# A deformable convolution with fewer columns in its edge tiles, and another order of work for its first image

## The chip, the cores and the metric

The kernel runs on one core of a Trainium2 chip. The metric is the device time of one execution in microseconds (us). The profile comes from one execution of its own. The engines are named as in the profile: PE (TensorE; PEld is its weight load), DVE (VectorE), ACT (ScalarE), POOL (GpSimd) and SP (SyncE, which here only issues DMAs).

## What is computed

Eight images of 128 channels and 64 x 64 pixels pass two layers. The first is a deformable convolution behind a group norm: an ordinary 3 x 3 convolution gives, for each pixel and each of nine taps, an offset in y, one in x and a mask; each tap then samples the image at its shifted place with bilinear weights, and a 1 x 1 product per tap sums the samples. The second layer is a mixture of four 3 x 3 convolutions, and the change doesn't touch it. Cut to what matters:

```python
def _deform_conv(x, off_w, off_b, w, b):
    om = conv(x, off_w, pad=1) + off_b[None, :, None, None]      # 27 rows
    off = om[:, :2 * KK].reshape(B_, KK, 2, H_, W_)
    mask = jax.nn.sigmoid(om[:, 2 * KK:])
    py = off[:, :, 0] + (jnp.arange(H_) - 1.0)[:, None] + ky
    px = off[:, :, 1] + (jnp.arange(W_) - 1.0)[None, :] + kx
    y0, x0 = jnp.floor(py), jnp.floor(px)
    ly, lx = py - y0, px - x0
    val = corner(y0, x0, (1 - ly) * (1 - lx)) + corner(y0, x0 + 1, (1 - ly) * lx) \
        + corner(y0 + 1, x0, ly * (1 - lx)) + corner(y0 + 1, x0 + 1, ly * lx)
    val = val * mask[:, None]
    return einsum('bckhw,ock->bohw', val, w) + b      # then batch norm, relu

x = x + _L0_conv_ref(_gn(x), ...)     # the deformable layer
x = x + _L1_conv_ref(_gn(x), ...)     # the mixture of experts
```

## The kernel before

Sampling is done as a matrix product. An image has 11 bands of T = 6 rows (NT1 = 11), a band 11 tiles of 6 columns. A tile looks at a window of Q = 10 by 10 pixels (6 and a reach of 2 to each side), which makes QQ = 100 rows of a contraction. Each of its 6 x 6 base positions has nine taps: 324 columns. The weight of a window pixel for a column is a product of two "tents", one of the y distance (times the mask) and one of the x distance.

The tables. `tables(b)` (L230) is a generator that makes the tents of image b, and the main loop takes a step of it at each tile (two at each third), so that its work lies between the tiles of an earlier image. For image 0 it runs to its end before the first tile (L622). It loads the image (L245), normalises it (L257 to L286), and computes the offset convolution in `combine` (L312, DVE) and `tap` (L329, PE); the result is `om`. ACT makes a copy of it with x and y exchanged (L375). Both are written to DRAM, by row (L378) and by column (L382), and read back (L397 for y offsets and masks, L405 for x offsets) with one image row or column per partition, a tap's values shifted by its place, into parts of the tile combo1. Then come five steps i, one for each pixel distance: ACT makes x tents in two instructions (L453 Abs, L460 Relu), DVE y tents in three (L458, L461, L463), and SP stores both to the DRAM tables taby and tabx (`store`, L431).

The bands. `load_y` (L471, six DMAs a band, POOL) and `load_x` (L485, ten DMAs) fetch a band's tents with each row repeated for the window pixels. `pick` (L503, ACT) cuts the windows out of the image, and `pixels` (L521) turns them on PE (L529) and copies them out of PSUM on ACT (L536). There is one PSUM buffer for this, ps_t. `weights` (L540, DVE) multiplies tents of x and y to `s`, three tiles ahead. `sample` (L554) multiplies window by weights on PE (L557) into one of three PSUM buffers `pq`, and ACT copies that to the tile `samples` (L563), which the convolution product of the band before reads (`conv`, L572, nine of 384 columns). A copy on ACT (L665) carries two rows from one band's samples to the next. Convolved rows go to DRAM (L590).

The order is the program's own: instructions stand on each engine in the order in which the loop at L640 issues them, and a DMA on SP, ACT or POOL also waits for the eighth DMA before it of its kind. The column order of a tile is (tap, row, column): `x_wts` is read with a step over base columns a, and y with step 1:

```python
x_wts[g % 3][0:QQ, c].rearrange("p a k r -> p k r a"),
y_wts[g % 2][0:QQ, :, :, T * c : T * c + T].rearrange("p r k a -> p k r a"),
```

Base positions run over 66 x 66 and not 64 x 64, since a tap's row and column are put at the place the convolution will ask for. So at an image's border some taps of the outermost base positions are computed and never read.

Of the kernel before, what the change touches and what calls it, by code (L numbers as in the profile page):

```python
# [16 lines left out]
P = 128  # L17
# [3 lines left out]
TAPS = 9  # L21
# [36 lines left out]
def deform_moe_conv(  # L58
# [110 lines left out]
    def dense():  # L169

        with ExitStack() as st:
# [15 lines left out]
            for t in picked:  # L187
# [18 lines left out]

            combos = [a1.tile([P, H // 2, W], F32, name=f"combo{i}") for i in range(2)]
# [3 lines left out]
                    "p (u v j) -> p u v j", u=3, v=3  # L211
                )
                for i in range(2)
            )
            off_x = flat[0:WB, 2 * YSTEP : 2 * YSTEP + TAPS * (WP6 - 1) + ROWPAD]


            x_wts = [a1.tile([P, NT1, T, TAPS, T], F32, name=f"xwts{i}") for i in range(3)]
            y_wts = [a1.tile([P, T, TAPS, WB], F32, name=f"ywts{i}") for i in range(2)]
# [3 lines left out]
            samples = [a1.tile([P, TAPS, T + 2, WB], F32, name=f"samples{i}") for i in range(2)]  # L223
            dw_sb = a1.tile([P, TAPS, P], F32, name="dw_sb")
            ystats = a1.tile([P, B, NT1, 6], F32, name="ystats")
            ymvs = a1.tile([P, B, 2], F32, name="ymvs")
            xts, ss = {}, {}
            bands = [(b, j) for b in range(B) for j in range(NT1)]

            def tables(b):  # L230
# [11 lines left out]
                others = (nc.sync, nc.sync) if b else (nc.scalar, nc.gpsimd)  # L242
# [132 lines left out]
                nc.scalar.copy(omc, omr.rearrange("p (h w) -> p w h", w=W))  # L375
                yield from pause(4)
                for j in range(4):
                    nc.sync.dma_start(  # L378
                        out=rowwise[b][:, j * HW // 4 : (j + 1) * HW // 4],
                        in_=omr[32 * j : 32 * j + 27],  # L380
                    )
                    others[j % 2].dma_start(  # L382
                        out=colwise[b][:, :, H // 4 * j : H // 4 * (j + 1)],
                        in_=omc[32 * j + 9 : 32 * j + 18],
                    )
# [3 lines left out]
                if b == 0:  # L389
                    for t in (y_wts[1], x_wts[1], x_wts[2]):  # L390
                        nc.vector.memset(t, 0.0)
                yield from pause(9)
                for k in range(3):
                    rows = slice(k, k + H)
                    for t, c in ((off_y, 3 * k), (mask, 2 * TAPS + 3 * k)):
                        one = t[rows, 0, k, 0:1]
# [3 lines left out]
                                ap=[list(one.ap[0]), [3 * WB + 1, 3], [1, W]],  # L400
# [3 lines left out]
                    one = off_x[rows, k * 3 * (WP6 - 1) + ROWPAD :]  # L404
                    others[k % 2].dma_start(  # L405
                        out=bass.AP(
                            tensor=one.tensor, offset=one.offset,
                            ap=[list(one.ap[0]), [WP6, 3], [1, H]],
# [9 lines left out]
                else:  # L418
                    tents = []
                    for t in samples:  # L420
                        flat = t.rearrange("p k r w -> p (k r w)")
# [4 lines left out]
                by_bands = bass.AP(  # L426
                    tensor=one.tensor, offset=one.offset,
                    ap=[list(one.ap[0]), [T, NT1], [WP6 - 1, TAPS], [1, T]],
                )

                def store(i):  # L431
# [8 lines left out]
                    )  # L440
                    nc.sync.dma_start(
# [8 lines left out]
                for i in range(NR):  # L450
                    ty, tx = tents[0][i], tents[1][i]
                    step = steps[0:WB, i : i + 1]
                    nc.scalar.activation(  # L453
                        tx.rearrange("p (n k j) -> p n k j", n=NT1, j=T), by_bands, AF.Abs, bias=step
                    )

                    dy, at = off_y.rearrange("p u v j -> p (u v j)"), REACH - i
                    nc.vector.tensor_scalar(ty, dy, -1.0, float(1 - at), ALU.mult, ALU.add)  # L458
                    yield
                    nc.scalar.activation(tx, tx, AF.Relu, bias=1.0, scale=-1.0)  # L460
                    nc.vector.scalar_tensor_tensor(ty, dy, float(1 + at), ty, ALU.add, ALU.min)  # L461
                    yield
                    nc.vector.scalar_tensor_tensor(  # L463
                        ty, ty, 0.0, mask.rearrange("p u v j -> p (u v j)"), ALU.max, ALU.mult
                    )
                    if i:
                        store(i - 1)
                    yield from pause(2)
                store(NR - 1)

            def load_y(g, r, engine):  # L471

                if g >= len(bands):
# [3 lines left out]
                    out=y_wts[g % 2][r * Q : (r + NR) * Q, r].rearrange("p b c -> p (b c)"),  # L477
# [62 lines left out]
            def weights(n):  # L540

                if n >= len(bands) * NT1:
                    return
                g, c = divmod(n, NT1)
                s = a6.tile([P, TAPS, T, T], F32, name="s")
                nc.vector.tensor_tensor(  # L546
                    s[0:QQ],
                    x_wts[g % 3][0:QQ, c].rearrange("p a k r -> p k r a"),
                    y_wts[g % 2][0:QQ, :, :, T * c : T * c + T].rearrange("p r k a -> p k r a"),
# [4 lines left out]
            def sample(n):  # L554
                g, c = divmod(n, NT1)
                pq = ps_q.tile([P, TAPS, T, T], F32, name="pq")
                nc.tensor.matmul(  # L557
                    pq.rearrange("p k r a -> p (k r a)"),
                    lhsT=xts[g][0:QQ, c],
                    rhs=ss.pop(n)[0:QQ].rearrange("p k r a -> p (k r a)"),  # L560
                    start=True, stop=True,
                )
                nc.scalar.copy(samples[g % 2][:, :, 2 : T + 2, T * c : T * c + T], pq)  # L563

            def conv(g, i, py):
# [4 lines left out]
                n = 3 * kx + ky  # L570
# [4 lines left out]
                    rhs=samples[g % 2][:, n, first + ky : T + ky, kx : kx + W],  # L575
# [16 lines left out]
            LOADS = 17  # L592
            made, later = tables(0), tables(1)
            for _ in range(LOADS):
                next(made)
            nc.sync.dma_start(out=offw_sb[:, :, 0:27], in_=off_w)
            for j in range(4):
                nc.sync.dma_start(
                    out=offb_sb[32 * j : 32 * j + 27], in_=off_b.rearrange("a s -> s a")
                )  # L600
            def reach():
# [5 lines left out]
                count = a1.tile([1, 1], F32, name="count")  # L607
                nc.vector.tensor_reduce(count, pn[0:1], AX.X, ALU.add)
                nc.vector.tensor_copy(count_i, count)
# [5 lines left out]
            for u in offu_sb:  # L615
                nc.gpsimd.tensor_scalar(u, u, 0.5, None, ALU.mult)
# [5 lines left out]
            for _ in made:  # L622
                pass
# [621 lines left out]
```

## Time and profile before

| | |
|---|---|
| three executions | 1700.83, 1702.66, 1706.56 us |
| the profiled execution | 1705.5 us, of which the span of the instructions is 1703.8 |
| PE busy in the span | 1591.8 us (93%) |
| DVE, ACT, POOL busy | 1280.1, 954.9, 938.3 us |
| sampling matmuls (L557, PE) | 1936 records, 693.5 us: two passes for each of 968 tiles |
| convolution matmuls (L572, PE) | 1584 records, 624.4 us |
| tile weights (L546, DVE) | 968 of 761 ns |
| copies out of PSUM (L563, ACT) | 968 of 443 ns |
| granted TensorE clock, mean | 0.973 |

A group's line in the profile names source line, engine, operation, what is written and read, the shape, how often, busy time and the mean of one; behind the bar stands the time for which the engine was idle before these instructions, and what ended the wait. A matmul of this data type is recorded twice, once for each pass, and the records of consecutive matmuls overlap, so that the distance from start to start tells more than the length. In an answer by windows each row is a stretch of time with the busy time of each engine in it.

### The profile page before, as it was taken

The page shows a single profiled execution, that of the slowest core. Times are in us where ns is not written, and L with a number is a line of the kernel's source. Part 1 is how long each engine was busy: PE and PEld are TensorE (multiplying, and loading weights), DVE is VectorE, ACT ScalarE, POOL GpSimd, SP SyncE. Part 2 cuts the span into 40 slices and gives each one's busy share as a digit, 9 for nine tenths or more (in the row PEclk, how much of TensorE's full clock was granted, in tenths as well). Part 3 has the DMA queues.
Part 4 walks back from the last instruction along what each step waited for, and adds up shares of the span by engine and source line. Part 5 has one row for each costly group of instructions (what it writes and reads, how often), then busy time and mean ns, then how long its engine had stood idle before and what let it go on. Part 6 is the DMA issues. An engine that isn't in the chain of part 4 may idle for free. (4 is left out here: it accounts for less than half of the span.)

```text
span 1703.8 us, 20572 instructions
## 1 busy us (share of the span) xinstructions
PE 1591.8 (93%) x6106; PEld 918.3 (54%) x6106; DVE 1280.1 (75%) x1990; ACT 954.9 (56%) x1970; POOL 938.3 (55%) x1518
## 2 busy tenths in 40 slices
PE   3299999999999999999999999999999479999998
PEld 1155565666566556656665665566665234444443
DVE  6586777678687868776786878686664888888882
ACT  1465765776576667657765766676664423333320
POOL 3375576658667757766686676667771412222210
PEclk9599999999999999999999999999999689999999
DMA  4644864685477457647854775675762624444111
GB/s 133 128 119 113 166 169 114 143 183 132 112 159 183 115 120 184 154 114 141 192 125 110 161 183 126 129 162 133 171 149 53 266 87 155 158 153 149 76 63 52
DMA packets 197598, 235.82 MB, mean 138 GB/s; under 512 B 133964, under 2 KB 148048, under 8 KB 197478
## 3 DMA queue, kind: packets, MB, share of 16 engines
q0 software_dynamic: 94976, 124.94, 33.4%
q1 hardware_dynamic: 100556, 109.04, 21.6%
q8 instruction: 54, 0.88, 0.2%
q10 hardware_dynamic: 1946, 0.41, 0.1%
q14 instruction: 66, 0.54, 0.1%
HBM read 183.00 MB, written 50.82 MB: 137 GB/s over the span
## 5 line engine op out<-in xcount | busy, mean ns | idle before, releaser
L546 DVE TENSOR_TENSOR s<-xwts,ywts 100x324 f32<-100x324 f32 x968 | 706.6, 761 | 205.3 <-PE pq L557 172.3
L557 PE MATMUL pq<-s,xt 100*128 100x324 f32 x1936 | 693.5, 440 | 6.0 <-DVE s L546 6.0
L563 ACT COPY samples<-pq 128x324 f32<-128x324 f32 x968 | 425.1, 443 | 410.1 <-PE pq L557 403.5
L572 PE MATMUL py<-samples,dw_sb 128*128 128x384 f32 (+1 forms) x1584 | 624.4, 476 | 0.7 <-ACT y L583 0.7
L492 POOL DMA_DIRECT2D xwts<-tabx x863 | 524.7, 618 | 74.0 <-DMA ywts<-taby 35.9
L476 POOL DMA_DIRECT2D ywts<-taby x528 | 302.9, 588 | 337.2 <-DVE s L546 259.6
L557 PEld LDWEIGHTS pq<-s,xt 100*128 100x128 f32 x1936 | 324.5, 190 | 163.5 <-issue 28.7
L572 PEld LDWEIGHTS py<-samples,dw_sb 128*128 128x128 f32 x1584 | 299.9, 189 | 135.1 <-ACT y L583 2.7
L529 PE MATMUL pt<-ident,picked 128*100 128x128 f32 x968 | 194.6, 276 | 44.2 <-ACT picked L516 34.6
L529 PEld LDWEIGHTS pt<-ident,picked 128*100 128x100 f32 x968 | 121.0, 128 | 186.9 <-issue 44.8
L1159 PE MATMUL pc<-v,u 128*128 128x512 f32 x384 | 172.5, 598 | 9.3 <-DVE u L1108 9.3
L1159 PE MATMUL pc<-v,wmix 128*128 128x512 f32 x384 | 176.0, 604 | 0.0
L536 ACT COPY xt<-pt 100x512 f32<-100x512 f32 (+1 forms) x264 | 147.7, 559 | 2.2 <-PE pt L529 2.2
L1159 PEld LDWEIGHTS pc<-v,u 128*128 128x128 f32 x384 | 72.4, 190 | 98.3 <-issue 85.1
L1137 ACT ACTIVATE t<-pc,bmix 128x512 f32<-128x512 f32 x32 | 22.0, 687 | 182.3 <-PE pc L1159 100.3
L586 DVE BATCH_NORM_STATS2 ystats<-y 128x6 f32<-128x384 f32 (+1 forms) x88 | 48.3, 549 | 100.4 <-ACT y L583 100.4
L1159 PEld LDWEIGHTS pc<-v,wmix 128*128 128x128 f32 x384 | 72.3, 191 | 88.4 <-issue 84.7
L508 ACT COPY picked<-pad 128x900 f32<-128x900 f32 x88 | 91.6, 1041 | 9.6 <-DMA xwts<-tabx 9.6
L665 ACT COPY samples<-samples 128x1188 f32<-128x1188 f32 x80 | 95.9, 1199 | 0.0
L987 POOL TENSOR_TENSOR x<-x,xt 128x512 f32<-128x512 f32 x32 | 47.3, 1514 | 85.0 <-ACT x L985 85.0
L312 DVE TENSOR_TENSOR combo<-pad 128x1024 f32<-128x1024 f32 x64 | 77.4, 1227 | 8.5 <-PE pc L329 8.5
L987 POOL TENSOR_TENSOR pad<-pad,pad 128x512 f32<-128x512 f32 x28 | 39.6, 1445 | 71.7 <-ACT pad L985 71.5
(145 smaller groups left out, 998.3 us busy)
## 6 DMA issues: line engine op xcount, KB each, us to landing
ywts<-taby POOLq DMA_DIRECT2D x528, 116.0 KB, 4.2
pad<-in_x_dram SPq DMA_DIRECT2D x48, 512.0 KB
xwts<-tabx POOLq DMA_DIRECT2D x173, 116.0 KB, 4.1
out_dram<-yo SPq DMA_DIRECT2D x32, 512.0 KB
xwts<-tabx POOLq DMA_DIRECT2D x172, 92.8 KB, 4.0
yd<-y SPq DMA_DIRECT2D x80, 192.0 KB
xwts<-tabx POOLq DMA_DIRECT2D x173, 69.6 KB, 3.7
pad<-yd SPq DMA_DIRECT2D x16, 512.0 KB
```

What stands on the lines that cost most here:

```text
L476: engine.dma_start(out=y_wts[g % 2][r * Q : (r + NR) * Q, r].rearrange("p b c -> p (b c)"), in_=bass.AP(tensor=y_table[b].tensor, offset=y ...
L492: engine.dma_start(out=x_wts[g % 3][q:QQ:Q, :, lo:hi].rearrange("p t a b c -> p t (a b c)"), in_=bass.AP(tensor=x_table[b].tensor, offset= ...
L508: nc.scalar.copy(picked[g % 2][:, 1 : NT1 - 1], bass.AP(tensor=one.tensor, offset=one.offset, ap=[list(one.ap[0]), [T, NT1 - 2], [W, Q], [ ...
L529: nc.tensor.transpose(pt[0:QQ, c], picked[g % 2][:, c0 + c].rearrange("p y x -> p (y x)"), ident,)
L536: nc.scalar.copy(xts[g][0:QQ, c0 : c0 + n], pt[0:QQ, 0:n])
L546: nc.vector.tensor_tensor(s[0:QQ], x_wts[g % 3][0:QQ, c].rearrange("p a k r -> p k r a"), y_wts[g % 2][0:QQ, :, :, T * c : T * c + T].rear ...
L557: nc.tensor.matmul(pq.rearrange("p k r a -> p (k r a)"), lhsT=xts[g][0:QQ, c], rhs=ss.pop(n)[0:QQ].rearrange("p k r a -> p (k r a)"), star ...
L563: nc.scalar.copy(samples[g % 2][:, :, 2 : T + 2, T * c : T * c + T], pq)
L572: nc.tensor.matmul(py[:, first:], lhsT=dw_sb[:, 3 * ky + kx], rhs=samples[g % 2][:, n, first + ky : T + ky, kx : kx + W], start=(i == 0), ...
L665: nc.scalar.copy(samples[g % 2][:, :, 0:2], samples[(g - 1) % 2][:, :, T : T + 2])
L987: adder.tensor_tensor(y, y, xt[:, c * CH : (c + 1) * CH], ALU.add)
L1159: nc.tensor.matmul(pc, lhsT=us[j][:, kx], rhs=vs[g][:, rows, kx : kx + W], start=(kx == 0), stop=(kx == 2),)
```

## The change

It has two parts. Every tile's columns get another order: (row, tap row) by (base column, tap column), with the tap column innermost, in tables, weights and PSUM. With the taps in reverse order (the weights and biases of the offset convolution are reversed by small copies at the start), the columns at the border that nobody reads lie at the ends, and `sample` leaves them out: a tile in the first or last band has two of 18 rows fewer, one at the left or right end two of 18 columns fewer. The copy to `samples` exchanges the last two dimensions, so that the samples of one tap lie side by side along w, and at the ends it takes a second, small copy. The last y tent step becomes three instructions, one for each tap column.

The second part is for image 0: the loads of offsets and masks go to places that don't overlap; the x offsets all come on ACT's queue; the exchange copy is shared by ACT and DVE; the sigmoid's table is loaded at the start; the x tents of the first three bands come first and have stores of their own; the y tables are stored alone; the x loads of band 0 are issued before the last y tent, `pick` and `pixels` of band 0 before the rest; and the stores of the other x tents stand between the x loads of band 1.

```diff
-                    "p (u v j) -> p u v j", u=3, v=3
+                    "p (v u j) -> p v u j", u=3, v=3
...
+            tent_y = combos[0].rearrange("p h w -> p (h w)")[0:WB, 0:YSTEP]
...
-            x_wts = [a1.tile([P, NT1, T, TAPS, T], F32, name=f"xwts{i}") for i in range(3)]
-            y_wts = [a1.tile([P, T, TAPS, WB], F32, name=f"ywts{i}") for i in range(2)]
+            x_wts = [a1.tile([P, NT1, T, T, TAPS], F32, name=f"xwts{i}") for i in range(3)]
+            y_wts = [a1.tile([P, T, 3, WB, 3], F32, name=f"ywts{i}") for i in range(2)]
...
-            samples = [a1.tile([P, TAPS, T + 2, WB], F32, name=f"samples{i}") for i in range(2)]
+            samples = [a1.tile([P, T + 2, 3, 3, WB], F32, name=f"samples{i}") for i in range(2)]
...
+            nc.scalar.activation(count_f, nhalf[0:1], AF.Sigmoid)
...
-                others = (nc.sync, nc.sync) if b else (nc.scalar, nc.gpsimd)
+                beside = nc.sync if b else nc.gpsimd
...
-                nc.scalar.copy(omc, omr.rearrange("p (h w) -> p w h", w=W))
+                turned = omr.rearrange("p (h w) -> p w h", w=W)
+                if b:
+                    nc.scalar.copy(omc, turned)
+                else:
+                    nc.scalar.copy(omc[:, 0 : W // 2], turned[:, 0 : W // 2])
+                    nc.vector.tensor_copy(omc[:, W // 2 :], turned[:, W // 2 :])
...
-                    rows = slice(k, k + H)
+                    rows = slice(2 - k, 2 - k + H)
...
-                by_bands = bass.AP(
+                by_bases = bass.AP(
                     tensor=one.tensor, offset=one.offset,
-                    ap=[list(one.ap[0]), [T, NT1], [WP6 - 1, TAPS], [1, T]],
+                    ap=[list(one.ap[0]), [1, WB], [WP6 - 1, 3], [3 * (WP6 - 1), 3]],
                 )
...
+                def tent_y_of(i):
+                    for v in range(3):
+                        nc.vector.scalar_tensor_tensor(
+                            tents[0][i].rearrange("p (v j u) -> p v j u", v=3, u=3)[:, v],
+                            tent_y.rearrange("p (v u j) -> p v j u", u=3, v=3)[:, v], 0.0,
+                            mask[:, v].rearrange("p u j -> p j u"), ALU.max, ALU.mult,
+                        )
...
+                early, rest = slice(0, FIRST * T), slice(FIRST * T, WB)
+                for i in range(NR):
+                    distance_x(i, early)
+                    tent_x(i, early)
+                for i in range(NR):
+                    for _ in distance_y(i):
+                        pass
+                    tent_y_of(i)
+                    store_y(i)
+                    if i == 1:
+                        for n in range(FIRST):
...
+                            nc.sync.dma_start(out=bass.AP(...), in_=bass.AP(...))
+                    if i == NR - 2:
+                        for q in range(5):
+                            load_x(0, q, nc.gpsimd if q % 2 else nc.sync)
+                for q in range(5, Q):
+                    load_x(0, q, nc.sync)
+                pick(0)
+                for _ in pixels(0):
+                    pass
+                for i in range(2):
+                    distance_x(i, rest)
+                    tent_x(i, rest)
+                for r in range(T):
+                    load_y(0, r, nc.gpsimd if r < 4 else nc.scalar)
+                pick(1)
+                for i in range(2, NR):
+                    distance_x(i, rest)
+                    tent_x(i, rest)
+                nc.vector.memset(x_wts[2], 0.0)
+                for r in range(T):
+                    load_y(1, r, nc.gpsimd)
+                for q in range(Q):
+                    load_x(1, q, nc.sync)
+                    if q % 2:
+                        i = q // 2
+                        nc.sync.dma_start(...)
...
-                    x_wts[g % 3][0:QQ, c].rearrange("p a k r -> p k r a"),
-                    y_wts[g % 2][0:QQ, :, :, T * c : T * c + T].rearrange("p r k a -> p k r a"),
+                    x_wts[g % 3][0:QQ, c].rearrange("p a r (y x) -> p (r y) a x", x=3),
+                    y_wts[g % 2].rearrange("p r y a x -> p (r y) a x")[
+                        0:QQ, :, T * c : T * c + T
+                    ],
...
+                asked = (
+                    slice(None),
+                    slice(2 * (j == 0), 3 * T - 2 * (j == NT1 - 1)),
+                    slice(2 * (c == 0), 3 * T - 2 * (c == NT1 - 1)),
+                )
+                pq = ps_q.tile([P, 3 * T, 3 * T], F32, name="pq")
                 nc.tensor.matmul(
-                    pq.rearrange("p k r a -> p (k r a)"),
+                    pq[asked],
                     lhsT=xts[g][0:QQ, c],
-                    rhs=ss.pop(n)[0:QQ].rearrange("p k r a -> p (k r a)"),
+                    rhs=ss.pop(n)[0:QQ].rearrange("p m a x -> p m (a x)")[asked],
                     start=True, stop=True,
                 )
-                nc.scalar.copy(samples[g % 2][:, :, 2 : T + 2, T * c : T * c + T], pq)
+                rows = samples[g % 2].rearrange("p r y x w -> p (r y) x w")
+                by_columns = pq.rearrange("p m (a x) -> p m x a", x=3)
+                m0, m1 = 2 * (j == 0), 3 * T - 2 * (j == NT1 - 1)
+                parts = [(slice(0, 3), int(c == 0), T - (c == NT1 - 1))]
+                if c == 0:
+                    parts.append((slice(2, 3), 0, 1))
+                if c == NT1 - 1:
+                    parts.append((slice(0, 1), T - 1, T))
+                for x, lo, hi in parts:
+                    nc.scalar.copy(
+                        rows[:, 6 + m0 : 6 + m1, x, T * c + lo : T * c + hi],
+                        by_columns[:, m0:m1, x, lo:hi],
+                    )
...
-                    rhs=samples[g % 2][:, n, first + ky : T + ky, kx : kx + W],
+                    rhs=samples[g % 2][:, first + ky : T + ky, 2 - ky, 2 - kx, kx : kx + W],
...
+            FIRST = 3
...
+            nc.sync.dma_start(out=raw_w.rearrange("p k s t -> p k (s t)"), in_=off_w)
+            nc.sync.dma_start(out=raw_b.rearrange("p s t -> p (s t)"), in_=off_b)
...
+            for k in range(TAPS):
+                nc.scalar.copy(reversed_w[:, :, :, k], raw_w[:, :, :, TAPS - 1 - k])
+            for k in range(TAPS):
+                nc.scalar.copy(reversed_b[:, :, k], raw_b[:, :, TAPS - 1 - k])
             for j in range(4):
+                nc.sync.dma_start(out=offb_sb[32 * j : 32 * j + 27], in_=offb_row)
...
-                nc.gpsimd.tensor_scalar(u, u, 0.5, None, ALU.mult)
+                nc.scalar.activation(u, u, AF.Copy, scale=0.5)
```

## The prediction

> **What bounds the kernel now.** I read the page's 40 slices first, then the windows by stage, the timeline of one steady band, the windows of the eleven bands of one image, and last the timeline of the start.
>
> ```profile
> PE   3299999999999999999999999999999479999998
> ```
>
> Two slices (85 us) at the start in which TensorE hardly works, then thirty full ones. The windows by stage:
>
> ```profile
> core 0: us, PE busy (x) PEld busy (x) DVE busy (x) ACT busy (x) POOL busy (x), PEclk, DMA share, GB/s
> 0.00:32.80 32.80, 16.13 (x100) 6.64 (x100) 20.02 (x30) 4.90 (x6) 12.20 (x38) 1.00 0.45 150
> 32.80:75.50 42.70, 3.07 (x11) 1.78 (x11) 20.04 (x20) 15.05 (x22) 11.81 (x20) 0.54 0.58 110
> 86.20:1306.00 1219.80, 1211.30 (x5119) 745.82 (x5118) 924.66 (x1371) 811.55 (x1754) 813.14 (x1372) 1.00 0.63 143
> ```
>
> From 86 to 1306 us PE is busy 99.3%: it is the bound of the banded stage. From 32.8 to 75.5 nothing is busy for even half the time: that is a chain of latencies. After 1306 the change touches nothing. In a steady band:
>
> ```profile
> 601.26 0.71 PE L557 MATMUL pq<-s,xt 100*128 100x324 f32 x2
> 601.81 0.81 PE L572 MATMUL py<-samples,dw_sb 128*128 128x384 f32 x2
> 602.46 0.38 PE L529 MATMUL pt<-ident,picked 128*100 128x128 f32 x2
> ```
>
> Starts count here, since ends overlap. 324 columns take 0.55 us until the next start, 384 take 0.65: 1.69 ns a column for both passes, with no fixed part. Fewer columns are time. Now bands 1, 6, 7, 8, 9 of image 3:
>
> ```profile
> 559.00:570.70 11.70, 11.31 (x53) 8.31 (x52) 9.96 (x18) 10.54 (x23) 9.18 (x14) 1.00 0.44 107
> 635.30:648.40 13.10, 13.10 (x53) 8.43 (x52) 9.75 (x16) 10.39 (x24) 10.75 (x19) 1.00 0.82 163
> 648.40:661.60 13.20, 13.20 (x53) 8.36 (x52) 12.58 (x21) 11.74 (x25) 6.66 (x12) 1.00 0.65 149
> 661.60:675.40 13.80, 13.19 (x52) 8.31 (x51) 11.07 (x17) 9.84 (x23) 9.24 (x16) 1.00 0.97 212
> 675.40:688.50 13.10, 13.10 (x53) 8.42 (x52) 8.54 (x13) 8.58 (x21) 7.79 (x13) 1.00 0.90 224
> ```
>
> The fourth figure is ACT: 8.6 us in a plain band, 11.74 in the band that also makes tents, of 13.1 that PE needs. ACT is second everywhere, and full in one band of an image; PE idles only there and in band 1 (0.6 and 0.4 us). The start:
>
> ```profile
> 45.64 0.47 DVE L458 TENSOR_SCALAR samples<-combo 66x594 f32<-66x594 f32 x1 [0.45 <-issue]
> 57.35 0.29 SPq L433 DMA_DIRECT2D taby<-samples  x1
> 58.67 18.54 SPq L492 DMA_DIRECT2D xwts<-tabx  x14
> 62.56 3.43 POOL L476 DMA_DIRECT2D ywts<-taby  x6 [19.70 <-DMA tabx<-samples]
> 75.49 4.73 DVE L546 TENSOR_TENSOR s<-xwts,ywts 100x324 f32<-100x324 f32 x7 [18.16 <-DMA ywts<-taby]
> ```
>
> Tents from 45.6, last y store 57.4, first y load 62.6, first weights 75.5.
>
> [...] L546 (x read with a step of 54 words) takes 761 ns for 324 elements, while contiguous L1107 takes 552 for 384; and ACT shows the like, since L375 (step 64) takes 2.00 us for 1024 elements where L665 takes 1.20 for 1188. [...]
>
> **The change, part by part.**
>
> *Columns.* An edge tile asks 288 of 324 columns, and a corner 256. Of 121 tiles of an image, 9 bands lose 2 x 36 = 72 columns, the first and last 9 x 36 + 2 x 68 = 460: 1568 an image, 12,544 in all, times 1.69 ns = 21.1 us off PE. PE being the bound, all of it is on the path unless another engine now ends later.
>
> *Weights on DVE (L546).* x now comes in runs of three and the output stays contiguous; [...]I take 0.57. That is 11 x 0.19 = 2 us of DVE a band, hidden behind PE: no time won.
>
> *y tents on DVE.* The last step becomes three of 198 elements with both sources hopping[...], overlapping to 1.35, in place of 0.69 (start to start). Five an image cost 3.3 us, about 2.3 in the tent band; DVE there stands at 12.58 and loses 2 through the weights: 12.9 under PE's 13.0. Nothing, narrowly.
>
> *x distances on ACT.* They now read with a step of 207 words: from L375 (2.00 - 0.2)/1024 = 1.76 ns an element against 0.83, so 0.82 becomes 1.37 us. Four fall in the tent band: +2.2. The edge tiles' extra copies (16 or 18 elements; L516's 70 cost 0.15 start to start) add 0.3. ACT there: 11.74 + 2.2 + 0.3 = 14.2 against PE's 13.1: 1.1 late. The pixel transposes have one PSUM buffer, so a late ACT stops PE soon (today's 0.6 us idle is just that wait, on ACT xt L536). I charge 1.1 us in each of the 7 images that make tents for a later one: +8.
>
> *The sample copies on ACT (L563).* They now read PSUM with a step of three words, 968 times. Below: 0.44 us as today. Above: every element pays what an SBUF hop costs ACT, 324 x 0.93 = +0.30, 0.74 us. Below today is excluded, since today's read is contiguous. I take 0.44: TensorE writes those words in this trace at one per 0.84 ns a pass[...]. It is a judgement; the upper end makes the main rival.
>
> *The first image.* Up to the offsets (32.8 us) little moves: eighteen small copies on ACT (about 0.15 us each) must wait for off_w, then four bias DMAs for them, and the first combine on DVE (15.39) for those DMAs, because they read combos[0]. With off_w there by 9.5, copies to 12.3, issue and landing 3.5 us, it is 0 to 0.7 late. The six offset and mask loads no longer wait for one another (36.6 to 44.9 today with gaps): issued by 41.5, landed by 43.5, y tents from 43 instead of 45.6. Each now takes 2.66 us instead of 2.0: the last at 43 + 13.3 = 56.4, not 57.3. So this is worth only 1 us. What follows is worth more: no x store lies in front of the last y store, which needs about 3.2 us instead of 5.2 (the first, alone, took 2.1), so y loads begin at 59.7; nine x loads stand in SP's queue before or beside it and are out by then. Four y loads on POOL and two on ACT are issued in 2.4 us and land 4 to 5.7 later: first weights at 66.5 against 75.5, that is 9 us. Queued behind on SP: ten x loads of band 1 and five x stores, 15 x 0.8 = 12 us from 61 plus 4 to land, 77; band 1 asks for them at 66.5 + 10.3 = 76.8. ACT's late distances (five of 1.7 us, the last ending about 68) hold up the first sample copies by under 1 us. I take 8.5 off, with 3 to 12 as bounds.
>
> *Sum.* -21.1 + 8 - 8.5 = -21.6. The profiled execution took 1705.5 us (span 1703.8 and 1.7 around it): 1684. The three runs have a median of 1702.66, 0.17% less: 1681.
>
> **Rivals.**
>
> *A, the sum above*: 1681, chance 0.40. *B, the tent band holds*: ACT's excess is taken up by the bands beside it (8.5 of 13) and the 8 us don't come: 1673; for it, PE waits little on ACT today; against it, the single transpose buffer. 0.15. *C, the start gives little*: the longer DVE tents, or SP's queue, where a DMA waits for the eighth before it and landings take 6.9 us (the median under load), eat most of it; column gain and stalls stand: 1690. 0.13.
>
> *D, the copies cost something*, 0.55 us: 1.2 us more ACT a band. Band 1 is then at 10.54 + 0.3 + 1.2 = 12.0 against 11.2, band 7 at 15.4 against 13.1; 3.1 an image, 22 in seven; -21.1 + 22 - 8.5: 1695. 0.12.
>
> *E, ACT becomes the bound (slower).* One mechanism: the PSUM read with a step pays the full hop, 0.74 us. Then a band carries 3.3 + 0.3 more: band 1 14.1 against 11.2, band 6 14.0 against 13.0, band 7 17.5 against 13.1, band 8 (with one late distance) 14.0 against 13.1; 9.2 us an image, 64 in seven; -21.1 + 64 - 8.5 = +35: 1738. It decides from about +0.16 us a copy (0.60), where 4.2 us an image eat up the 29.6 won. For it: both other engines' rows show what hops cost; against it: those are SBUF rows. 0.20.
>
> **How the numbers follow.** Predicted: 1681, with its own range of 1672 to 1692. A to D hold 0.80 of the chance and their tails lie outside, so the range reaches into E's lower part: 1666 to 1725. About 0.3% (5 us) is what a measurement of this kernel can tell from no change. Faster: A, B, C and most of D, 0.75; same: the rest of D, 0.05; slower: E, 0.20.
>
> **What would show it.** Columns: the sampling matmuls in groups of 324, 288 and 256 columns, starts 0.55, 0.48 and 0.43 us apart. Copies: their mean, 0.44 or 0.74; and in the waits whether sampling matmuls or transposes wait for ACT. Weights near 0.57. Tent band: ACT about 14 us of it. Start: y loads near 60, weights near 66, the first convolution about 8.5 us earlier than 90.6. I am wrong if ACT's share in plain bands passes 12 us, or if the weights still wait past 70 us.

## The result and the profile after

| | before | after |
|---|---|---|
| median of four executions | 1703.47 us | 1696.43 us |
| span of the profiled execution | 1703.8 us | 1695.0 us |
| band 2 begins (its first sampling matmul) | 100.65 us | 99.69 us |
| from there to the start of the last band | 1197.39 us | 1191.23 us |

The ratio is 0.9958 (95% interval 0.9940 to 0.9976): 7 us faster, where 21.6 were forecast. In the profiled execution 8.8 us go: 1.0 before band 2, 6.2 in the bands, 1.7 after the start of the last one (0.7 of it that band's own cut columns). The other 1.0 says nothing: this last stretch takes 399.2 to 404.1 us in the traces below that multiply the same columns.

First the groups of the changed kernel by shape: busy time, mean of one, idle time ahead and its cause.

```profile
L649 DVE TENSOR_TENSOR s<-xwts,ywts 100x324 f32<-100x324 f32 x968 | 456.7, 491 | 366.4 <-PE pq L670 333.0 <-DMA xwts<-tabx 12.0 <-DMA tabx<-samples 10.4
L685 ACT COPY samples<-pq 128x324 f32<-128x324 f32 x648 | 292.8, 456 | 261.3 <-PE pq L670 255.8
L470 ACT ACTIVATE work<-combo,steps 66x594 f32<-66x594 f32 x35 | 48.8, 1394 | 0.6 <-DVE s L649 0.6
L492 DVE SCALAR_TENSOR_TENSOR work<-combo,combo 66x198 f32<-66x198 f32 x105 | 33.8, 374 | 8.3 <-ACT combo L429 8.2
```

The copy out of PSUM, the large risk of the prediction, takes 456 ns for 443. The weights fall from 761 to 491 ns. The x distances cost ACT 1.39 us for 0.82, as foreseen. Then the windows of bands 1, 6, 7, 8, 9 of image 3:

```profile
554.43:566.04 11.61, 11.23 (x52) 8.26 (x51) 8.23 (x19) 10.55 (x25) 11.01 (x19) 1.00 0.54 138
630.56:643.54 12.98, 12.98 (x53) 8.33 (x51) 7.41 (x18) 10.38 (x23) 9.43 (x16) 1.00 0.87 158
643.54:657.38 13.84, 13.38 (x53) 8.26 (x51) 12.51 (x33) 13.84 (x29) 8.43 (x14) 1.00 0.69 166
657.38:671.64 14.26, 13.16 (x52) 8.29 (x51) 6.05 (x14) 10.37 (x26) 10.16 (x19) 1.00 0.93 210
671.64:684.62 12.98, 12.98 (x53) 8.32 (x52) 5.74 (x13) 8.65 (x23) 8.85 (x15) 1.00 0.88 226
```

Plain bands are 0.07 us shorter than before, where 0.12 were counted. The tent band (third row) has ACT full, 13.84 of 13.84, and PE idle for 0.46; in the band after it PE loses another 1.1. What PE waits for there, by the waits of its weight load in these two bands:

```profile
PEld pt L632 <- ACT xt L639: 3.1, 3, 1.6
```

Three transposes wait for ACT's copy of the one before (total, times, longest). Last the start, in order of time (what ended an engine's idle time stands in brackets):

```profile
59.91 2.08 ACTq L579 DMA_DIRECT2D ywts<-taby  x2
60.47 4.53 POOL L579 DMA_DIRECT2D ywts<-taby  x8 [6.41 <-DMA taby<-samples]
...
65.04 0.31 SPq L562 DMA_DIRECT2D tabx<-samples  x1
...
69.92 1.55 SPq L595 DMA_DIRECT2D xwts<-tabx  x2
70.32 2.53 DVE L649 TENSOR_TENSOR s<-xwts,ywts 100x324 f32<-100x324 f32 x6 [10.44 <-DMA tabx<-samples]
...
76.56 3.41 SPq L595 DMA_DIRECT2D xwts<-tabx  x2
...
85.11 0.49 DVE L649 TENSOR_TENSOR s<-xwts,ywts 100x324 f32<-100x324 f32 x1 [5.56 <-DMA ywts<-taby]
```

The y loads begin at 60 as predicted. The first weights come at 70.3 (forecast 66.5). And there is a second hole that the sum hadn't: band 1's first weights stand still for 5.6 us until 85.1. The last of its x loads is issued only at 79 to 80 us and lands at 84.9; the profile puts the wait down to a y load, but the y loads of that band had all been issued by 68.3 and had landed by 72.8. (In the same way it puts the first weights' wait down to a store; of band 0's loads the last to land, at 69.9, is ACT's second y load.) SP's own waits from 60 to 86 us say why its queue is late:

```profile
SPq L595 <- DMA ywts<-taby: 4.5, 1, 4.5
SPq L562 <- DMA ywts<-taby: 2.3, 1, 2.3
```

SP issues x loads (L595) and stores (L562), yet it waits for *y* loads: the two that ACT issued at 59.9. In this program a DMA waits for the eighth before it, and SP and ACT share that count: in the trace their DMAs use the same eight semaphores in turn (100, 102, 103, 105, 106, 107, 109 and 110), POOL's use eight others (111 to 118), and SP's x load at 69.9 waits for 106, the one of ACT's second y load. So the two y loads, slow to land, held up band 1's x loads by 6.8 us.

### The profile page after: what moved, and what is told of

Its sections match the earlier page's. It is cut to its first block, busy times and chain, and to the rows that moved or that the text cites. A ratio compares the mean times of both kernels' runs of the same rounds, so it can differ in the third digit from the quotient of the medians.

```text
span 1695.0 us, 20897 instructions
## 1 busy us (share of the span) xinstructions
PE 1579.0 (93%) x6106; PEld 914.2 (54%) x6106; DVE 1044.2 (62%) x2071; ACT 979.5 (58%) x2176; POOL 937.1 (55%) x1518
## 5 line engine op out<-in xcount | busy, mean ns | idle before, releaser
L670 PE MATMUL pq<-s,xt 100*128 100x324 f32 (+2 forms) x1936 | 674.9, 430 | 19.1 <-DVE s L649 19.1
L649 DVE TENSOR_TENSOR s<-xwts,ywts 100x324 f32<-100x324 f32 x968 | 456.7, 491 | 366.4 <-PE pq L670 333.0
L685 ACT COPY samples<-pq 128x324 f32<-128x324 f32 (+5 forms) x1144 | 437.1, 405 | 395.7 <-PE pq L670 389.2
L595 POOL DMA_DIRECT2D xwts<-tabx x862 | 524.7, 617 | 106.5 <-DMA ywts<-taby 41.1
L632 PE MATMUL pt<-ident,picked 128*100 128x128 f32 x968 | 196.4, 278 | 36.4 <-ACT picked L619 19.5
L632 PEld LDWEIGHTS pt<-ident,picked 128*100 128x100 f32 x968 | 116.3, 129 | 180.9 <-issue 65.9
L1280 PEld LDWEIGHTS pc<-v,wmix 128*128 128x128 f32 x384 | 72.3, 191 | 88.6 <-issue 84.9
L786 ACT COPY samples<-samples 128x1188 f32<-128x1188 f32 x80 | 96.9, 1211 | 0.0
```

The costliest lines, as they stand in the source:

```text
L595: engine.dma_start(out=x_wts[g % 3][q:QQ:Q, :, lo:hi].rearrange("p t a b c -> p t (a b c)"), in_=bass.AP(tensor=x_table[b].tensor, offset= ...
L632: nc.tensor.transpose(pt[0:QQ, c], picked[g % 2][:, c0 + c].rearrange("p y x -> p (y x)"), ident,)
L649: nc.vector.tensor_tensor(s[0:QQ], x_wts[g % 3][0:QQ, c].rearrange("p a r (y x) -> p (r y) a x", x=3), y_wts[g % 2].rearrange("p r y a x - ...
L670: nc.tensor.matmul(pq[asked], lhsT=xts[g][0:QQ, c], rhs=ss.pop(n)[0:QQ].rearrange("p m a x -> p m (a x)")[asked], start=True, stop=True,)
L685: nc.scalar.copy(rows[:, 6 + m0 : 6 + m1, x, T * c + lo : T * c + hi], by_columns[:, m0:m1, x, lo:hi],)
L786: nc.scalar.copy(samples[g % 2][:, 0:2], samples[(g - 1) % 2][:, T : T + 2])
```

## Experiments

"Band 2" is the time at which band 2 begins; "bands" runs from there to the start of the last band. The nine kernels with the changed kernel's start put band 2 between 98.8 and 102.3, and where the code of the bands is the same (the changed kernel, `c_in`, `c_out` and the four of the start) they come out within 0.9 us of each other. A difference in "bands" below 0.9 us is not read, and one of a few us in "band 2", from one trace each, is read with care. Spans also hold the last stretch, which varies by 4.9 us, so they are not compared on their own.

| | ratio to the kernel before (95%) | span | band 2 | bands |
|---|---|---|---|---|
| the changed kernel | 0.9958 (0.9940-0.9976) | 1695.0 | 99.7 | 1191.2 |
| c_full | 1.0039 (1.0024-1.0054) | 1709.0 | 99.6 | 1206.4 |
| c_rows | 0.9998 (0.9983-1.0012) | 1702.4 | 102.3 | 1197.7 |
| c_in | 0.9950 (0.9933-0.9967) | 1691.1 | 101.4 | 1190.5 |
| c_out | 0.9955 (0.9941-0.9968) | 1692.5 | 99.6 | 1190.5 |
| c_even | 0.9944 (0.9933-0.9956) | 1692.9 | 100.9 | 1189.6 |
| t_flat | 0.9885 (0.9855-0.9916) | 1681.7 | 100.2 | 1177.4 |
| t_pause | 0.9943 (0.9926-0.9961) | 1689.5 | 100.4 | 1186.9 |
| t_dve | 0.9883 (0.9846-0.9920) | 1680.6 | 98.8 | 1179.5 |
| s_second_undone | 0.9933 (0.9914-0.9953) | 1691.4 | 96.7 | 1190.6 |
| s_pool | 0.9954 (0.9936-0.9973) | 1690.2 | 97.5 | 1190.5 |
| s_split | 0.9910 (0.9875-0.9945) | 1684.8 | 91.6 | 1191.2 |
| s_late | 0.9912 (0.9878-0.9946) | 1688.8 | 94.7 | 1190.4 |
| x_three | 0.9813 (0.9790-0.9835) | 1670.8 | 90.9 | 1177.5 |
| x_three_full | 0.9908 (0.9886-0.9931) | 1683.1 | 90.2 | 1192.6 |

### What the columns are worth

```diff
 c_full
-    pq[asked], ... rhs=...rearrange("p m a x -> p m (a x)")[asked],
+    pq, ... rhs=...rearrange("p m a x -> p m (a x)"),
 c_rows
-    slice(2 * (c == 0), 3 * T - 2 * (c == NT1 - 1)),
+    slice(None),
```

> The changed kernel, but every sampling matmul multiplies all 324 columns (the copies still take the asked ones). Theory 1 (the columns left out are worth 1.95 us an image, as the bands of the two traces say): about 15.6 us slower than the changed kernel, a plain band 13.05 us from start to start, the first band of an image 13.5, the last 13.05. Rival (the prediction's 1.69 ns for each of 12,544 columns, part of it lost in stalls elsewhere): 21 us slower, a plain band 13.10.

> The changed kernel, but only the first and last band's rows are left out of the matmul (contiguous columns), the left and right edge's columns are multiplied. Theory 1 (a cut in rows saves its full 1.69 ns a column, a cut at the left or right edge only about 60% of it, because the pattern then breaks into 18 runs of 16): plain band 13.05, first and last band as in the changed kernel to 0.05 us, some 5 us slower than the changed kernel in all. Rival (every column left out is worth the same): first and last band 0.10 us longer than in the changed kernel, plain bands 0.12 longer, some 10 us in all.

With all columns multiplied a plain band takes 13.09 us, which is *more* than the 13.05 of the kernel before; in `c_rows`, where only rows are cut and a plain band so keeps all its columns, 13.09 as well. So the columns cut at the left and right edge save 0.11 of the 0.12 us that were forecast, the rival's value and not mine: comparing bands of the two kernels had misled me, because a second, opposite effect of 0.04 us a band lies over it. The total, 15.1 us in the bands, is still near theory 1's 15.6, since bands 2, 7 and 8 take the same time with all their columns as without (17.46, 13.84 and 14.27 us for 17.46, 13.83 and 14.29; means over six images). c_rows' bands are 6.5 us longer than the changed kernel's, between the 5 and the 10 expected.

```diff
 c_in
+    nm, nk = 3 * T - 2 * (j in (0, NT1 - 1)), 3 * T - 2 * (c in (0, NT1 - 1))
-    rhs=...rearrange("p m a x -> p m (a x)")[asked],
+    rhs=...rearrange("p m a x -> p (m a x)")[:, 0 : nm * nk] (as p m k),
 c_out
-    pq[asked],
+    pq.rearrange("p m k -> p (m k)")[:, 0 : nm * nk] (as p m k),
```

> The changed kernel, but the edge tiles' matmuls read their 288 or 256 weights as one contiguous piece (other weights than the right ones); the result in PSUM keeps its runs of 16. Theory 1a (the reading of runs costs TensorE about one more cycle a run and pass): a plain band falls from 12.98 to about 12.93 us, the kernel gains 3 to 5 us on the changed one. Theory 1b (the writing to PSUM costs it): no difference, 12.98.

> The changed kernel, but the edge tiles' results lie packed in PSUM (one contiguous piece of 288 or 256 columns), the weights are read in runs of 16 as before; the copies read the packed piece. Theory 1a (reading costs): no difference, plain band 12.98. Theory 1b (writing to PSUM costs): plain band 12.93, 3 to 5 us faster than the changed kernel.

Neither moves a plain band (12.98 in both). Theory 1 is gone: broken patterns cost the matmul nothing here. What the 0.04 us are is seen when the starts of a plain band's matmuls are laid side by side (band 9 of image 3, worked out from the traces: ns from the start of one record to the next; q sampling, pt transposes, py convolution, "..." a cut; `c_even` and `x_three` come below):

```
before   q275 q271 pt112 pt108 q275 q272 ... py325 py322 q276 q272 py325 py321 q276 q272 py325 py321
c_full   q275 q272 pt112 pt108 q275 q272 ... py326 py321 q276 q272 py331 py329 q275 q272 py325 py321
after    q246 q241 pt122 pt109 q277 q271 ... py326 py321 q275 q272 py330 py329 q275 q272 py325 py322
c_even   q245 q242 pt121 pt109 q277 q271 ... py326 py321 q275 q271 py325 py323 q274 q272 py325 py322
x_three  q245 q242 pt135 pt109 q277 q272 ... py326 py322 q275 q271 py325 py322 q275 q272 py325 py321
```

An edge tile's two passes fall by 30 ns each for 36 columns, 1.67 ns a column as reckoned; some 10 to 23 ns of it come back in the transpose behind the left tile. But each third convolution, the one with the middle tap column, now takes 330 + 329 ns for 325 + 322. Three a band are 0.04 us. Its samples begin at an odd word, as before, but their rows now lie 594 words apart and not 66.

```diff
 c_even
-    rows[:, 6 + m0 : 6 + m1, x, T * c + lo : T * c + hi],          (planes 66 words apart)
+    planes[:, 6 + m0 : 6 + m1, :, T * c + lo : T * c + hi],        (planes 65 words apart)
...
-    rhs=samples[g % 2][:, first + ky : T + ky, 2 - ky, 2 - kx, kx : kx + W],
+    rhs=flat[:, first + ky : T + ky, 2 - ky, at : at + W],          (at = (2 - kx) * 65 + kx)
```

> The changed kernel, with the three column planes of the samples 65 words apart and not 66, so that every convolution reads its runs of 64 from an even word. Theory 4 (in the changed kernel each third convolution, the one that reads from an odd word, takes 330 ns a pass for 325 or 322, since its rows now lie 594 words apart and not 66): all convolutions take 322 to 326 ns, a plain band 12.94 and not 12.98 us, 3 us faster than the changed kernel. Rival (the distance between the rows does it, whatever the start): the third convolutions stay at 330, plain band 12.98.

All convolutions of that band take 321 to 327 ns, and a plain band 12.94 us. So an odd start together with rows far apart is what costs; the distance stays and the price is gone. The whole is worth 1.6 us in the bands and not 3, since bands 1, 2, 7 and 8 don't profit: there PE isn't all that counts.

### The tent band

```diff
 t_flat
-    by_bases[:, bases], AF.Abs, ...
+    (one[:, 0 : TAPS * WB] as p w y x if b else by_bases)[:, bases], AF.Abs, ...
 t_pause
-    yield from pause(2)
+    yield from pause(4)
```

> The changed kernel, but the x distances of images 1 to 7 read the offsets as they lie (contiguous, so in another order than the tables want). Theory 3 (ACT's backlog in the tent band, 1.39 in place of 0.82 us each, makes the transposes late): the distances take 0.8 us again, bands 7 and 8 of an image give back 1.1 us, 8 us faster than the changed kernel. Rival (DVE, busy for 12.5 us of the tent band, or the loads of that stretch hold it): bands 7 and 8 stay within 0.3 us, nothing won.

> The changed kernel, with a pause of four steps and not two between the tents of images 1 to 7, so that they reach into the next band, where ACT is busy for 10.4 of 14.3 us. Theory 3: no backlog, PE idles under 0.3 us in bands 7 and 8 together (now 1.6), 8 to 11 us faster than the changed kernel. Rival (the stall moves to the band after, or the tables come too late for POOL's loads): less than 3 us won.

With a contiguous read bands 7 and 8 of image 3 look so:

```profile
637.94:651.04 13.10, 13.10 (x52) 8.26 (x51) 11.93 (x31) 12.68 (x30) 8.09 (x14) 1.00 0.71 171
651.04:664.02 12.98, 12.98 (x52) 8.31 (x51) 6.61 (x16) 9.09 (x24) 9.15 (x17) 1.00 0.91 222
```

2.0 us an image come back, 13.8 in all, more than the 8 expected: the stall that the kernel before had in band 8 (0.6 us) goes too. Why that one goes no run shows apart; DVE has 6.6 us of work there where it had 11.1. DVE's y tents don't hold PE: DVE has 11.9 of 13.1 us, and PE has no idle time. The pause gives 0.6 us an image, 4.3 in the bands, so neither the 8 to 11 of theory 3 nor the rival's under 3: ACT then has 12.5 and 12.1 us in bands of 13.5 and 14.0 and is nowhere full, and PE still waits for its copies. So it isn't ACT's total alone. In the trace of `t_pause` the longest of these waits (1.1 us, ended at 661.7) stands behind a run of ACT work without a gap: from 657.5 a distance (1.36 us), the carry copy L786 (1.21), the second step of a tent (0.72), with sample copies between, and only then the copy that the transpose needs. That the order of this work is to blame fits, but no run tests the order by itself.

```diff
 t_dve (with t_pause's edit)
+    if b:
+        nc.vector.tensor_scalar(one, one, 1.0, 0.0, ALU.subtract, ALU.min)
+        return
...
-    nc.scalar.copy(xts[g][0:QQ, c0 : c0 + n], pt[0:QQ, 0:n])
+    nc.scalar.activation(xts[g][...], pt[...], AF.Copy, scale=-1.0 if bands[g][0] else 1.0)
```

> The changed kernel, with the second step of the x tents of images 1 to 7 on DVE (the least of distance minus one and nought, so negative; the pixel copies turn the sign back) and the pause of four steps. Theory 3 (ACT's backlog ahead of the transposes' copies): ACT loses 0.75 us a tent, bands 7 and 8 take 13.0 to 13.2 each, 11 to 14 us faster than the changed kernel. Rival (DVE becomes the bound, with 0.5 us a tent more on about 12): the weights come late, bands 7 and 8 stay at 27.5 us or more together, as with the pause alone.

```profile
638.36:651.41 13.05, 13.05 (x52) 8.34 (x51) 11.79 (x31) 10.74 (x25) 7.41 (x13) 1.00 0.57 143
651.41:664.50 13.09, 13.09 (x53) 8.26 (x52) 10.31 (x25) 10.76 (x25) 8.66 (x15) 1.00 0.72 172
```

PE has no idle time in either band, and DVE carries the step (468 ns by `x_three`'s groups) without holding PE: 11.8 us in the bands, as theory 3 says, with the hop left in place. So taking time off ACT, by either of two ways, takes the stall away.

### The start

```diff
 s_second_undone: image 0's tents as for the others, then
+    load_y(0, r) on POOL; load_x(0, q) on SP, ACT, POOL in turn; load_y(1, r) on POOL; load_x(1, q) on SP
 s_pool
-    load_y(0, r, nc.gpsimd if r < 4 else nc.scalar)
+    load_y(0, r, nc.gpsimd)
```

> The changed kernel, but the first image's tents, stores and loads go in the order of the kernel before (all tents of x and y in step, y and x stores in turn, then the loads); the offset loads stay apart from one another. Theory 2 (in the changed kernel the first weights do come earlier, but band 1 waits for its x loads, so that next to nothing is left): first weights near 74.5, band 1 within 1.5 us of the changed kernel's 85.8, the same time as the changed kernel to 2 us. Rival (the prediction: the order is worth 7.5 us): band 1 at 92 to 93, 7 us slower.

> The changed kernel, with the last two y loads of band 0 on POOL's queue behind the other four, not on ACT's. Theory 2a (SP's x loads of band 1 stand still from 65.4 to 69.9 us because the next of them may only go when ACT's second y load has landed; eight transfers are under way at most over SP and ACT together): SP issues band 1's x loads without that gap, the last lands near 79 and not at 84.9, band 1 begins near 81, 4 to 5 us are won. Theory 2b (the DMA engines are full and land the loads late in any order): the last x load lands at 83 or later, under 2 us won.

The expectation for the first was that undoing the order changes nothing. It *gains*: band 2 begins at 96.7, three us earlier than in the changed kernel and two earlier than in any of the nine, although the first sampling matmul comes three us later (73.9 against 70.9). In these traces the new order of tents, stores and loads was a loss; the ratios of the whole (0.9933 and 0.9958) go the same way, but their intervals overlap. What is certain is that it was not worth the 7.5 us of the rival. The windows of the changed kernel, then of s_second_undone, show where:

```profile
68.00:76.00 8.00, 5.13 (x13) 3.78 (x14) 3.66 (x9) 1.89 (x6) 6.26 (x11) 0.50 0.81 160
76.00:84.00 8.00, 4.70 (x21) 2.92 (x19) 3.55 (x7) 4.95 (x14) 4.58 (x8) 0.93 0.90 180
84.00:92.00 8.00, 6.25 (x19) 4.35 (x20) 6.29 (x14) 3.27 (x7) 4.73 (x8) 0.60 0.60 133
```

```profile
68.00:76.00 8.00, 2.13 (x6) 1.67 (x7) 2.52 (x6) 0.93 (x3) 4.36 (x8) 0.50 0.83 166
76.00:84.00 8.00, 7.16 (x26) 4.92 (x25) 6.13 (x12) 5.15 (x13) 5.34 (x11) 0.74 0.64 129
84.00:92.00 8.00, 7.58 (x37) 5.62 (x36) 6.24 (x17) 5.91 (x14) 7.92 (x14) 1.00 0.69 170
```

In the changed kernel the granted clock (third figure from the end) rises to 0.93, PE then stands for four us, and the clock falls to 0.60; s_second_undone starts later, doesn't stop, and has 1.00 from 84 on. Two losses go with the hole: its own 4.2 us, and a longer band 1, 13.9 us in the one and 12.1 in the other. The other traces agree. In ten of them (the nine and `s_pool`) PE stands for 3.0 to 7.7 us ahead of band 1; in all ten the clock then falls to 0.50 for 6.8 or 10.2 us, and band 1 takes 13.4 to 14.8 us. Where there is no such hole (`s_second_undone` and the later `s_split` and `x_three`) it takes 12.1 to 12.9. How much of the difference is the clock's alone isn't taken apart: the kernel before, with other weights, has no hole there and takes 13.7.

With the y loads on POOL, SP's x loads do go without the gap, but the last of them lands at 82.4 and band 1 begins at 83.5: 2.2 us won at band 2, between the two theories and no more than the scatter of equal starts. SP no longer waits for y loads, so they were what had held it. What is still late may be the full DMA engines (0.94 busy from 68 to 76) or the order in which they are used: band 2's loads from POOL are under way beside band 1's on SP. The next two runs tell these apart.

```diff
 s_split (with s_pool's edit)
+    for q in range(1, Q, 2):
+        load_x(1, q, nc.gpsimd)
     for r in range(T):
         load_y(1, r, nc.gpsimd)
     (on SP only the even q of load_x(1, q), and the five stores)
 s_late (with s_pool's edit)
     (the five stores behind all of load_x(1, q), not between them)
```

> The changed kernel, with all six y loads of band 0 on POOL, then every second x load of band 1 on POOL ahead of band 1's y loads, and only the other five on SP. Theory 2a (band 1's loads stand behind others on SP, and behind band 2's loads from POOL): band 1's last load lands by 78, no gap between bands 0 and 1, band 2 begins at 96 or earlier (99.7 in the changed kernel, 97.5 with the y loads on POOL). Theory 2b (the DMA engines are full whatever the order): band 2 begins at 97 or later.

> The changed kernel, with all six y loads of band 0 on POOL and the five late x stores behind all of band 1's x loads, not between them. Theory 2a: band 1's x loads are issued by 70 and landed by 77, band 2 begins at 96 or earlier; the late stores then hold up band 2's or 3's loads by under 1 us. Theory 2b: the last x load lands at 80 or later, band 2 begins at 97 or later.

s_split begins band 2 at 91.6, 8.1 us earlier than the changed kernel:

```profile
68.00:76.00 8.00, 6.97 (x25) 5.06 (x26) 6.09 (x13) 3.54 (x9) 5.33 (x10) 0.71 0.94 187
76.00:84.00 8.00, 6.75 (x28) 3.89 (x28) 7.10 (x17) 6.27 (x18) 7.51 (x13) 1.00 0.66 160
84.00:92.00 8.00, 8.00 (x39) 6.04 (x37) 4.25 (x12) 4.86 (x13) 8.00 (x15) 1.00 0.58 144
```

The DMA engines move about as much as in the changed kernel (187 and 160 GB/s for 160 and 180), only in the order in which it is wanted, and PE never stops for long. So theory 2b, that full DMA engines land the loads late in any order, is refuted: the order, what stands ahead of what, decides. s_late closes the first hole (band 1 at 79.3) and opens another: I expected under 1 us from the late stores, and band 1 takes 15.3 us, because ACT waits 4.7 us for them (PE stands for 2.7 us of it, and here the clock stays at 1.00). Image 0's tents lie in the tiles `samples`, which band 1's copies overwrite. First ACT's wait, then the window:

```profile
ACT samples L685 <- DMA tabx<-samples: 4.7, 1, 4.7
...
84.00:92.00 8.00, 6.42 (x29) 4.75 (x30) 3.02 (x10) 6.22 (x15) 7.12 (x13) 1.00 0.49 127
```

### All three together

> The changed kernel with three remedies at once: the loads of s_split, the tents of t_dve, the planes of c_even. If the three losses are apart from one another, their gains by the traces add: 8.1 + 12.9 + 3.2 = 24 us, a span near 1671, band 2 begins near 91.5, plain bands 12.95, bands 7 and 8 13.05 each. Rival (they share a cause, such as the DMA engines or DVE, and the gains overlap): a span of 1677 or more.

> The same as x_three, but every sampling matmul multiplies all 324 columns. What is left out is then measured where no other engine is late: if all of it lies on the path at 1.5 to 1.7 ns a column, 19 to 21 us slower than x_three. Rival (part of the cut tiles is hidden by waits): 16 us or less, as between the changed kernel and its full version (14 us).

The edits are those of s_split, t_dve and c_even, and for the second c_full's on top.

```profile
span 1670.8 us, 20921 instructions
...
L681 PE MATMUL pq<-s,xt 100*128 100x324 f32 (+2 forms) x1936 | 672.3, 429 | 13.9 <-DVE s L660 13.9
```

The span is 24.2 us less than the changed kernel's, where 24 were expected from adding. The agreement is better than the sum deserves: it put 12.9 and 3.2 for tents and planes, where the bands of `t_dve` and `c_even` show 11.8 and 1.6. With the 8.1 of the start these make 21.5 up to the start of the last band, and `x_three` gains 22.6 there (1268.3 for 1290.9); the rest of the 24.2 lies in the last stretch, which the edits hardly touch. So the three gains do add, to about 1 us: the losses are apart from one another. Its median is 1672.74 us, 1.9% under the kernel before (0.9790 to 0.9835). Without the cut, x_three_full's bands are 15.1 us longer, the rival's "16 or less". The cut's 0.72 and 0.69 us in an image's first and last band and 0.10 in plain ones come through; in band 2 (17.45 and 17.46 us) and band 7 (13.05 and 13.03) nothing does.

## Why the prediction was wrong

The forecast was 1681 us, 21.6 less than before, with its own range 1672 to 1692; 1696.4 was measured, 7.0 less, a third of it. Only the wide range (1666 to 1725), made so for rival E, holds the measured time. In number rival D (1695) is nearest, but by luck: it put a copy out of PSUM at 0.55 us, and it takes 0.456; D and E are gone. In mechanism rival C (the start gives little, through SP's queue and late landings) came true, though its 1690 still has the columns in full. The forecast's own sign of being wrong came too: the first weights waited until 70.3, and the first convolution stood at 90.0 us, for 90.6 before and about 82 forecast.

In the span 8.8 us went, 12.8 fewer than the 21.6. Of these, 7.5 are missing at the first image (8.3 with the first band's columns) and about 5.3 in the bands (11.5 forecast, as columns less stalls; 6.2 measured); the last stretch gave 0.9 more than its columns, within its scatter.

- *Columns, -21.1.* The price of a column was right (60 ns for 36). What failed is "all of it is on the path": between band 2 and the last band 15.1 us come through, where the forecast's columns for these bands make 19.5 (12,544 less the 992 of the two first and the last, times 1.69 ns). In bands 2 and 7 nothing of it comes through even in `x_three`, where ACT's stalls are gone, so these bands are not set by the sampling matmuls alone (what sets them no run shows), and a little returns in the transposes.
- *What the sum did not have.* The samples' new layout makes three of nine convolutions slower, 0.04 us a plain band; c_even gave back 1.6 us. The prediction priced the new patterns for DVE, ACT and PSUM, and never for the matmul that reads `samples`.
- *Stalls in the tent band, +8.* Right in size: 13.84 and 14.26 us for 13.2 and 13.8 before, so 1.1 an image. Right in the wait: transposes wait for ACT, which is full for 13.84 us where 14.2 was put. Right only in part in the reason: the forecast counted ACT's total in one band, and `t_pause` shows PE waiting where ACT isn't full. Rival B is refuted.
- *Copies out of PSUM at no cost.* Right: +13 ns, not +300. Nor does TensorE's writing suffer: runs of 16 (the changed kernel) and a packed piece (`c_out`) give the same band, 12.98 us. The edge tiles' second copy takes 202 ns and is hidden in plain bands, where PE is busy for 12.98 of 12.98 us (`c_full` has it too).
- *Weights and y tents on DVE.* No time lost through them, as said, but both were put too dear: weights 491 ns (570), a y tent step 374 ns (500). Both forecasts were my estimates, and no trace had shown a step like the y tents', whose two sources hop by 66 words. It comes to (374 - 155) / 198 = 1.1 ns an element, an estimate; its fixed part of 155 ns is worked out from two groups of the kernel before, 552 ns for 384 contiguous elements (L1107) and 769 for 594 (L461).
- *First image, -8.5.* This is the step that failed most: 1.0 us at band 2's start, part of it columns. The offset loads were issued by 44.4 and not 41.5, but the y tents still began at 44.2 (43 forecast) and the y loads at 59.9 (59.7). ACT's load of the sigmoid's table, 1.28 us at 46.5 in the kernel before, did move to the start (0.8 us). Then "land 4 to 5.7 later" was too short: the first weights came 3.8 us after the forecast's, when the last y load had landed at 69.9; the DMA engines were 0.86 busy from 60 to 68, but no run tests whether that is why. And "15 x 0.8 = 12 us from 61 plus 4 to land, 77" counted SP's issues only: SP stood still for 6.8 us behind ACT's two y loads, since one count of eight runs over both queues, and the last x load landed at 84.9. The rule of the eighth DMA was in the text, though only as a rival's reason. `s_split`, with band 2 at 91.6 for 100.7 before, shows that the 8.5 were there to be had.

## What to carry to other kernels

Price a new layout for each engine that reads or writes it, the matmul's moving operand included. When transfers are issued earlier, write down the whole queue of every issuer with what each entry waits for: here two loads on a spare queue held up ten on another, and in these traces a stage that started three microseconds earlier ended three later. Where a faster start leaves a hole soon after, look at the granted clock behind it: here it stood at half behind each of the ten holes of 3.0 us or more ahead of band 1.

## What was not expected of the hardware

- A PE that starts, then stands for 4.2 us, goes on at half the granted clock: 0.50 from 84 to 90 us in the changed kernel, 1.00 from 84 on without the hole (`s_second_undone`). Ten holes of 3.0 to 7.7 us were followed by this, `s_late`'s of 2.7 was not; where between them the limit lies, and whether the length alone decides, no run shows.
- Convolution reads of 64 words in rows 594 words apart take 5 to 8 ns a pass more from an odd word than from an even one; with rows 66 words apart the odd word costs nothing (325 and 322 ns).
- ACT reading SBUF with a step of 207 words takes 0.97 ns an element more than in runs of six, as the kernel before has them ((1394 - 816) / 594). The 0.83 ns and 0.2 us that the prediction sets against a step are near what the kernel before shows: 585 ns for 384 elements and 477 for 256 (L583) give 0.84 ns an element, which leaves 0.20 us of the 1.20 for 1188 (L665), an estimate. Reading PSUM with a step of three words, and writing in the new order, costs 13 ns in 324 elements (456 for 443).
- DVE reads runs of three words about as fast as contiguous ones: 491 ns for 324 products. In the kernel before 384 contiguous ones take 552 ns (L1107) and 594 take 769 (L461), so 1.03 ns an element; 60 fewer than 384 would make 490, an estimate.
